# Norm sums over the partitions for two channel chunks at once, and norm weights folded into the input projection, in a selective-scan and mixture-of-experts kernel on one Trainium2 core

## The chip, the cores and the metric

The kernel runs on one NeuronCore of one Trainium2 chip. Its engines run side by side, each through its own instructions in order: TensorE (PE, matrix products into PSUM, with the loads of its stationary operand listed apart as PEld), VectorE (DVE), ScalarE (ACT), GpSimd (POOL) and SyncE (SP, which issues most of the transfers). [...] The metric is the time of one execution on the device in microseconds. Before the change the median of three runs is 3180.68 us (3179.35 to 3183.71).

## The reference

Two layers, each followed by a layer norm without weights. The first is a selective state-space model on `x` of 8 sequences, 1024 time steps and 256 features. The second sends each of the 8192 tokens to two of eight experts of limited capacity. Cut to what matters here:

```python
var = jnp.mean(x * x, axis=-1, keepdims=True)
xn = x * jax.lax.rsqrt(var + 1e-06) * norm_w
proj = xn @ W_in.T                       # 256 -> 1024: x_branch and gate
...
def step(h, inp):                        # h: (B, 512 channels, 16 states)
    dA_t, dB_t, x_t, C_t, t = inp
    h = h * dA_t + dB_t * x_t[:, :, None]
    nrm = jnp.sqrt(jnp.sum(h * h, axis=(1, 2), keepdims=True))
    fac = jnp.minimum(20.0 / (nrm + 1e-08), 1.0)
    h = jnp.where(t % 10 == 0, h * fac, h)
    y = jnp.einsum('bdn,bn->bd', h, C_t) + D_param * x_t
    return (h, y)
```

At every tenth step the state of a sequence is scaled down when its norm, taken over all 512 channels and 16 states, exceeds 20. After the scan come the gating, the output projection, the residual, the layer norm and the experts.

## The kernel before

**Tiling.** Channels lie on the 128 partitions, in `NC` = 4 chunks. Time is cut into 52 windows of 20 steps (`TW`), each window into two stretches of 10 steps (`CH`), so that the norm falls between two stretches. The eight sequences form `G` = 2 groups of `NB` = 4. A unit is one stretch of one group; it has four scans on DVE, one for each chunk, each over 16 states x 4 sequences x 11 slots (`scan`, L968, L975, L980). A window has four units.

**Order.** Nothing is scheduled by a tool. Each piece of work is put on a list with a time written out by hand (`WHEN`, `FIRST`, `LAST`), in units of one scan, and the list is sorted; that fixes each engine's order. Windows overlap: while window w is scanned, the next one is normed, projected and convolved, and the one before is gated, projected out and normed.

**Set-up.** SP issues the transfers in this order: the small parameters `sm`, the first window's `x`, the first half of `w_in` (the x branch), the convolution's biases, `w_bc`, `w_dt`, the second half of `w_in` (the gate), `w_out`, the router's weights, and a fill of `seg_d` with zeros. DVE then builds the convolution's 16 diagonal matrices `taps` from the identity and `sm` (L510), and the small constants, among them `scl`: one DVE instruction (L523), an exponential on ACT (L524), and further DVE instructions. After them come the scalings of `w_dt_sb` and `w_bc_sb` (L530 to L532).

**One window, ahead of its scans.** `rms` squares and sums on ACT (L610), takes the power on POOL (L605, L606) and scales on ACT (L614). `turn` transposes on PE into a PSUM tile `ptr` (L625). `turned` copies it to SBUF, one ACT instruction for each of the two chunks of features, with the norm's weights as a scale for each partition (L635). `project` multiplies by `w_in_sb` (L647), in four parts: two for the x branch, two for the gate. `branch` copies the x branch on ACT (L664), `convolve` runs on PE (L692, L696), `convolved` on ACT and DVE (L709, L711). `find_bc`, `find_dt` (L718, L785) and what follows give the step widths; `tanhs` and `expand` on ACT (L851, L930) give the decays. `gate` is one ACT and one DVE instruction for each half (L681, L683). All PSUM tiles called `mm` share two buffers, so a new one waits for the reader of the one before the last.

**The norm of a unit.** `norm` has five steps at times of their own: the squares of the last states on POOL (L892); their sums over the partitions on PE, as products with a matrix of ones, one for each chunk, added up in one PSUM tile of 64 columns (L897); the sum over the 16 states on DVE, giving four numbers per partition (L904); scale and power -1/2 on POOL (L909, L910); a copy into PSUM on ACT (L914). The next unit of the same group reads it in L975. The norms ahead of the first scan are in `first_states`, with the squares on DVE.

**After the scans.** POOL multiplies by C (L998), PE sums over the states (L1017) and adds the skip term (L1026), DVE multiplies by the gate (L1031), and `leave` projects out, norms and writes (L1056 to L1147). Every 256 time steps a batch of routing runs, with indirect transfers on POOL's queue (L301).

## Time and profile before

One execution was profiled. Its own time was 3200.79 us and the span of its instructions 3199.1 us, beside the 3180.68 us median of the runs without profiling.

| | us |
|---|---|
| median of three runs | 3180.68 |
| profiled execution: time, span | 3200.79, 3199.1 |
| mean granted TensorE clock, share of full | 0.944 |
| scans on DVE, L980 x824 | 1327.7 |
| norm's sums on PE, L897 x1632, 128x64 each | 219.2 (0.280 each) |
| their idle time ahead on PE | 40.4 |
| norm's reduction on DVE, L904 x204 | 0.215 median each |
| copies of the transposed norm on ACT, L635 x104 | 0.393 median each |

A line of a timeline has the start, the duration, the engine, the source line, the operation with its output and inputs, their shapes, and how many instructions of the kind follow each other; in brackets the idle time of the engine ahead of it, and whose work ended that. A float32 product shows as two PE instructions, so four products are eight. In a table by stretches, each engine has its busy time and its instructions; then follow the granted clock of PE, the share of the transfer engines, and GB/s. In the list of waits the numbers are the total in us, the times it happened, and the longest.

### The profile page before, as it was taken

The numbers are of one execution on the slowest core, as the hardware profiler recorded it, in microseconds if no ns is written. First come the engines' busy times: TensorE is split into PE (matmuls) and PEld (weight loads), VectorE is DVE, ScalarE is ACT, GpSimd is POOL, SyncE is SP. The second block draws the span as 40 slices with busy tenths as digits, with TensorE's granted clock in tenths as the row PEclk, the third lists the DMA queues.
The fourth block names the chain that finished last, engine by engine and source line by source line (L and its number), as shares of the span: only waits on it lengthen the run. The fifth ranks groups of instructions, "written<-read, shape, count | busy, mean of one in ns | idle before, by whom it ended". The sixth has DMA issues, their size and how long they took to land. (4 is left out here: it accounts for less than half of the span.)

```text
span 3199.1 us, 53115 instructions
## 1 busy us (share of the span) xinstructions
PE 2804.9 (88%) x17774; PEld 2553.2 (80%) x17774; DVE 2606.0 (81%) x3954; ACT 2435.9 (76%) x6300; POOL 2421.1 (76%) x2801
## 2 busy tenths in 40 slices
PE   5889999898898999988898999998999988579998
PEld 5788888888788888888888888887888887457666
DVE  3899999998779999998899998998899998534444
ACT  6999899998778999988899988988898986011111
POOL 2777777788987777879987877789877876856663
PEclk8899999999899999999999999999999998789999
DMA  2122222223222222222222222222222221223331
GB/s 83 60 70 65 78 66 75 70 64 70 56 54 80 65 71 72 65 70 64 68 66 72 69 71 65 74 63 69 62 76 69 63 76 51 87 71 112 121 114 50
DMA packets 167102, 229.38 MB, mean 72 GB/s; under 512 B 52948, under 2 KB 105260, under 8 KB 166828
## 3 DMA queue, kind: packets, MB, share of 16 engines
q1 hardware_dynamic: 152236, 201.48, 21.2%
q0 software_dynamic: 14592, 24.52, 3.0%
q8 instruction: 139, 2.28, 0.3%
q14 instruction: 135, 1.11, 0.1%
HBM read 185.17 MB, written 40.63 MB: 71 GB/s over the span
## 5 line engine op out<-in xcount | busy, mean ns | idle before, releaser
L980 DVE TENSOR_TENSOR_SCAN U<-dA,u 128x704 f32<-128x704 f32 (+1 forms) x824 | 1327.7, 1611 | 42.6 <-DVE u L975 0.5
L998 POOL TENSOR_TENSOR U<-U,cb 128x640 f32<-128x640 f32 x816 | 1168.6, 1443 | 96.4 <-DMA cb<-c_d 93.5
L851 ACT ACTIVATE th<-dt,a 128x160 f32<-128x160 f32 (+1 forms) x3328 | 1146.3, 422 | 0.1
L1017 PE MATMUL py<-U,ident 128*128 128x160 f32 (+1 forms) x6592 | 1058.7, 312 | 55.1 <-DVE sg L1031 50.2
L1017 PEld LDWEIGHTS py<-U,ident 128*128 128x128 f32 x6592 | 973.1, 199 | 68.1 <-DVE sg L1031 57.6
L968 DVE TENSOR_TENSOR u<-pdt,bb 128x640 f32<-128x640 f32 (+1 forms) x824 | 677.9, 823 | 39.1 <-ACT pdt L914 23.0
L930 ACT ACTIVATE dA<-th 128x640 f32<-128x640 f32 (+1 forms) x824 | 595.3, 731 | 1.6
L647 PE MATMUL pp<-xnT,w_in_sb 128*128 128x168 f32 (+1 forms) x1664 | 299.4, 328 | 11.7 <-ACT xnT L635 11.7
L692 PE MATMUL pc<-xb,taps 128*128 128x168 f32 (+1 forms) x1664 | 275.9, 309 | 21.0 <-POOL xb L663 10.5
L647 PEld LDWEIGHTS pp<-xnT,w_in_sb 128*128 128x128 f32 x1664 | 273.3, 209 | 15.3 <-ACT xnT L635 15.3
L785 PE MATMUL pd<-xc,w_dt_sb 128*128 128x168 f32 (+1 forms) x1664 | 275.0, 322 | 0.0
L692 PEld LDWEIGHTS pc<-xb,taps 128*128 128x128 f32 x1664 | 249.4, 193 | 25.3 <-POOL xb L663 12.3
L785 PEld LDWEIGHTS pd<-xc,w_dt_sb 128*128 128x128 f32 x1664 | 255.8, 201 | 0.5 <-issue 0.5
L897 PE MATMUL total<-sq,ones 128*128 128x64 f32 x1632 | 219.2, 280 | 40.4 <-POOL sq L892 35.8
L897 PEld LDWEIGHTS total<-sq,ones 128*128 128x128 f32 x1632 | 216.3, 202 | 47.8 <-POOL sq L892 45.2
L975 DVE SCALAR_TENSOR_TENSOR u<-pdt,U 128x64 f32<-128x64 f32 x816 | 222.2, 272 | 28.2
L910 POOL TENSOR_TENSOR f<-f,mhalf 128x4 f32<-128x4 f32 x204 | 209.5, 1027 | 17.0
L892 POOL TENSOR_TENSOR sq<-U 128x256 f32<-128x256 f32 x204 | 131.8, 646 | 98.4 <-DVE U L980 81.0
L1056 PE MATMUL po<-w_out_sb,sg 128*80 128x256 f32 (+1 forms) x824 | 196.7, 382 | 0.3 <-DVE sg L1031 0.3
L1425 PE MATMUL ph<-xeT,w1s 128*128 128x384 f32 x512 | 172.0, 493 | 10.5 <-DVE hT L1431 4.5
L773 POOL TENSOR_SCALAR dx<-xc,hd 128x168 f32<-128x168 f32 (+1 forms) x208 | 179.1, 866 | 2.6 <-PE py L1026 2.6
L1455 PE MATMUL epo<-w2s,hT 128*128 128x256 f32 x768 | 171.8, 383 | 9.2 <-issue 4.7
(227 smaller groups left out, 3347.4 us busy)
## 6 DMA issues: line engine op xcount, KB each, us to landing
bb<-b_d SPq DMA_DIRECT2D x206, 320.0 KB
cb<-c_d SPq DMA_DIRECT2D x206, 320.0 KB
w1s<-in_w SPq DMA_DIRECT2D x8, 1024.0 KB
w2s<-in_w SPq DMA_DIRECT2D x8, 1024.0 KB
xt<-in_x SPq DMA_DIRECT2D x102, 80.0 KB
v<-in_x SPq DMA_DIRECT2D x102, 80.0 KB
x_d<-v SPq DMA_DIRECT2D x102, 80.0 KB
sum_d<-v SPq DMA_DIRECT2D x102, 80.0 KB
```

What stands on the lines that cost most here:

```text
L647: nc.tensor.matmul(pp[:, i * S : (i + 1) * S], w_in_sb[:, k, o * P : (o + 1) * P], r["xnT"][:, k * S : (k + 1) * S], start=(k == 0), stop= ...
L692: nc.tensor.matmul(out_c, taps[:, c * KCONV + k, :], r["xb"][:, c, k * B : k * B + S], start=(k == 0), stop=False,)
L785: nc.tensor.matmul(r["pd"][:, c % 2 * S : (c % 2 + 1) * S], w_dt_sb[:, k, c * P : (c + 1) * P], r["xc"][:, k * S : (k + 1) * S], start=(k ...
L851: nc.scalar.activation(r["th", c][:, i, : B * n].rearrange("p (b t) -> p b t", b=B), dtv[:, c, :, 1 : 1 + n], AF.Tanh, scale=a16[:, cn : c ...
L897: nc.tensor.matmul(v.total[:, : NS * NB], ones, v.sq[:, c * NS : (c + 1) * NS].rearrange("p n b -> p (n b)"), start=(c == 0), stop=(c == N ...
L910: nc.gpsimd.tensor_tensor(v.f, v.f, mhalf, ALU.pow)
L930: nc.scalar.activation(dA.rearrange("p (n b) t -> p n b t", b=NB)[:, :, :, 1 : 1 + su], th[:, :, g * NB : (g + 1) * NB, v.t0 : v.t0 + su], ...
L968: nc.vector.tensor_tensor(uv[:, :, :, 1 : 1 + su], dtx.unsqueeze(1).to_broadcast([P, NS, NB, su]), v.bb.rearrange("p (n b t) -> p n b t", ...
L975: nc.vector.scalar_tensor_tensor(uv[:, :, :, 0], p.pf.unsqueeze(1).to_broadcast([P, NS, NB]), 1.0, p.h_last[:, c * NS : (c + 1) * NS, :], ...
L980: nc.vector.tensor_tensor_scan(v.U[:, c * NS : (c + 1) * NS].rearrange("p x b t -> p (x b t)"), v.dA[c].rearrange("p x t -> p (x t)"), u, ...
L998: nc.gpsimd.tensor_tensor(cut.rearrange("p x b t -> p (x b) t"), cut.rearrange("p x b t -> p (x b) t"), cb, ALU.mult,)
L1017: nc.tensor.matmul(v.py, ident, Uc[:, :, n, :, 0:ty], start=(n == 0), stop=False)
```

## The change

Three edits. First, in the set-up, ahead of the taps, four DVE instructions multiply the two halves of `w_in_sb`, for each of the two chunks of features, by the norm's weights, in place. Second, `turned` is one copy of both chunks without a scale. Third, step 1 of `norm` multiplies the matrix of ones by the squares of two chunks at once, so two products of 128 columns take the place of four of 64; step 2 then sums over 32 columns for each sequence in place of 16.

```diff
+        for half in range(2):
+            for k in range(KM):
+                part = w_in_sb[:, k, half * NC * P : (half + 1) * NC * P]
+                nc.vector.tensor_scalar(part, part, sm[:, S_NW + k : S_NW + k + 1], None, ALU.mult)
+
         taps = wpool.tile([P, NC * KCONV, P], F32, tag="taps", name="taps")
...
             r["xnT"] = xnT = p2.tile([P, KM * B * TM], F32, tag="xnT", name=f"xnT_{w}")
-            for k in range(KM):
-                nc.scalar.activation(
-                    xnT[:, k * S : (k + 1) * S], r["ptr"][:, k * S : (k + 1) * S], AF.Copy,
-                    scale=sm[:, S_NW + k : S_NW + k + 1],
-                )
+            nc.scalar.copy(xnT[:, : KM * S], r["ptr"][:, : KM * S])
...
-                for c in range(NC):
+                for c in range(0, NC, 2):
                     nc.tensor.matmul(
-                        v.total[:, : NS * NB], ones,
-                        v.sq[:, c * NS : (c + 1) * NS].rearrange("p n b -> p (n b)"),
-                        start=(c == 0), stop=(c == NC - 1),
+                        v.total[:, : 2 * NS * NB], ones,
+                        v.sq[:, c * NS : (c + 2) * NS].rearrange("p n b -> p (n b)"),
+                        start=(c == 0), stop=(c + 2 == NC),
                     )
             elif step == 2:
                 v.f = p2.tile([P, NB], F32, tag="f", name=f"f_{v.nm}")
                 nc.vector.tensor_reduce(
-                    v.f, v.total[:, : NS * NB].rearrange("p (n b) -> p b n", b=NB), AX.X, ALU.add
+                    v.f, v.total[:, : 2 * NS * NB].rearrange("p (n b) -> p b n", b=NB), AX.X, ALU.add
                 )
```

## The prediction

> **What bounds the kernel now.** I read the page first, then the start instruction by instruction, then the waits of VectorE (DVE), then single windows of 20 time steps.

> ```profile
> PE 2804.9 (88%) x17774; PEld 2553.2 (80%) x17774; DVE 2606.0 (81%) x3954; ACT 2435.9 (76%) x6300; POOL 2421.1 (76%) x2801
> ...
> PE   5889999898898999988898999998999988579998
> ...
> DVE  3899999998779999998899998998899998534444
> ```

> By share of busy time TensorE (PE) leads. But its mean mixes the scan phase (slices 2 to 34) with the expert phase behind it. In the scan phase DVE shows the same nines, so the waits have to decide.

> ```profile
> DVE xc L711 <- ACT xc L709: 127.8, 95, 7.5
> ...
> DVE u L968 <- ACT pdt L914: 23.0, 28, 4.2
> DVE f L904 <- PE total L897: 13.3, 10, 2.9
> ```

> Over the whole run DVE waits only 13.3 us for the sums this change rewrites. Its one large wait is L711, once per window, and L711 waits for ScalarE (ACT). In the timelines DVE otherwise runs scan after scan. From the first L711 of a window to the gating product L683 always takes 30.7 us, without a gap. From there to the next L711 the time varies. Two neighbouring windows show why:

> ```profile
> 1177.60 1.35 PE L1017 MATMUL py<-U,ident 128*128 128x160 f32 x8 [1.17 <-DVE sg L1031]
> ...
> 1180.79 0.48 PE L625 MATMUL ptr<-ident,xn 84*128 84x84 f32 x4 [1.83 <-DVE f L904]
> ...
> 1182.93 2.28 PE L647 MATMUL pp<-xnT,w_in_sb 128*128 128x168 f32 x8
> ...
> 1185.25 0.44 ACT L664 COPY xb<-pp 128x336 f32<-128x336 f32 x1 [1.36 <-PE pp L647]
> ...
> 1200.31 0.51 DVE L711 SCALAR_TENSOR_TENSOR xc<-xc,pc 128x336 f32<-128x336 f32 x1 [1.75 <-ACT xc L709]
> ...
> 1286.03 1.30 PE L647 MATMUL pp<-xnT,w_in_sb 128*128 128x168 f32 x8
> ...
> 1300.42 0.50 DVE L711 SCALAR_TENSOR_TENSOR xc<-xc,pc 128x336 f32<-128x336 f32 x1 [0.67 <-ACT xc L709]
> ```

> L683 frees a PSUM buffer, PE transposes into it (L625), ACT copies (L635), PE projects (L647), ACT copies (L664) and then works without a gap up to L709, which releases L711. The eight L647 took 2.28 us in one window and 1.30 in the other, because the granted clock was 0.50 there:

> ```profile
> 1178.30:1181.50 3.20, 1.37 (x12) 1.15 (x12) 3.14 (x5) 2.59 (x8) 3.20 (x4) 1.00 0.05 19
> 1181.50:1184.90 3.40, 3.40 (x15) 3.40 (x14) 3.30 (x6) 2.39 (x7) 3.23 (x6) 0.50 0.02 5
> ```

> The half clock follows a stretch in which PE was busy for only 1.37 of 3.20 us. So a window lasts as long as DVE's work plus one pass through PE and ACT, and that pass depends on whether PE has just been idle. Of 34 windows without routing 9 last about 49.4 us (full clock), 7 about 50.35 (half clock at +14 us, which delays L785 and so ACT L799), 16 about 50.8 (half clock at the transposes) and 2 about 51.9 (half clock twice running, as at 1952 to 1959). The mean is 50.39.

> The start, up to the first scan at 57 us, is one chain:

> ```profile
> 4.32 3.22 DVE L510 TENSOR_SCALAR taps<-ident,sm 128x128 f32<-128x128 f32 x16
> ...
> 7.80 0.20 ACT L524 ACTIVATE scl<-scl 128x1 f32<-128x1 f32 x1 [4.68 <-DVE scl L523]
> ...
> 7.91 0.40 ACT L610 ACTIVATE xn<-xt 84x256 f32<-84x256 f32 x1
> ...
> 8.03 0.51 SPq L478 DMA_DIRECT2D w_in_sb<-in_w_in  x1
> ...
> 13.82 1.23 DVE L530 TENSOR_SCALAR w_dt_sb<-w_dt_sb 128x2048 f32<-128x2048 f32 x1 [5.17 <-DMA w_dt_sb<-in_w_dt]
> ```

> ACT cannot begin the first norm (L610) before L524, and L524 waits for DVE L523, which stands behind the taps in DVE's order.

> **Part 1, the four multiplications of w_in.** They go into DVE's order ahead of the taps. The first two need the first half of w_in, the last two the second half, whose transfer is issued at 8.03, behind w_dt's. When does it land? Adding up the bytes of one-microsecond stretches, everything up to w_dt (some 1,890 KB) had moved by 12.5 us, and w_dt was seen landed at 13.82, 1.3 later. The second half of w_in ends at some 2,420 KB, moved by 14.5; with the same lag it lands at 15.8. Bounds: not before 13.82 (same queue, behind w_dt), and not after w_out behind it, 2,940 KB at 16.1, so 17.4. One multiplication of 128x512: 128 elements took 0.22 us (L531) and 2048 took 1.23 (L530), so 512 lie at 0.42; the taps, which take their factor from a column as these do, cost 0.06 more: 0.48. Two of them follow the landing, some 0.9 us; the first two are hidden by the wait (another 0.9 without it). Then L523 comes 3.31 behind the first tap and L524 0.17 later, as now: 15.8 + 0.9 + 3.31 + 0.17 = 20.2 against 7.80, **+12.4 us** (10.4 to 14.0). Queued behind the wait on DVE are the taps, L523 and with it ACT's L524 and L610, hence the norm, the projection and all behind them. Nothing covers this: PE, POOL and ACT have no other work. What now waits at 13.82 for w_dt will no longer wait, but that was off the chain. SP's queue only issues earlier relative to use. No DMA is added.

> **Part 2, the first norms.** The two groups of L897 before the first scan ran at half clock, 1.97 and 1.94 us, and lie on the chain: the power behind them holds POOL up to 44.2, then L828, for which ACT L946 idles 4.70 us. Four instructions in place of eight: at least half the time (0.98), at most four times the 0.285 of the 168-column L647 at half clock (1.14). I take 1.1, a gain of 0.85 each; the longer reductions return 0.07 each. **-1.6 us** (-1.9 to -1.4).

> **Part 3, the norm's sums in every window** (four norms each, 204 in all). PE: eight L897 of 64 columns take 0.92 us from start to next start, 0.115 each; 160 columns take 0.136. So 128 columns lie between, I take 0.115 (the nearer row is the floor of the small ones): 0.46 saved, 94 us over the run; with 0.136, 0.38. [...]

> PE's saving mostly ends in a wait: L1017 and L625 wait for DVE already. DVE: the reduction reads 128 in place of 64 elements. L904 takes 0.209 now, reductions of 128x128 (L243, L254) 0.266 and 0.279: +0.07 us. The bound above is L390's strided 0.38, +0.17. Two of the four reductions lie in the gapless 30.7 us and lengthen the window by 0.14; the other two are covered by the L711 wait (0.67 at least; without that cover they cost as much again).

> **Part 4, one copy for two (L635).** Two activations take 0.69 us together, the like copy of 128x336 (L664) 0.44: ACT saves 0.25. It counts only where ACT is gapless from L635 or earlier to L709, which is the 49.4 and 50.35 kinds; in the others L664 waits for PE.

> **Windows, summed.** 49.4 becomes 49.3; 50.8 becomes 50.9; 51.9 becomes 52.0; 50.35 becomes about 49.65 (L785's second half stands behind an L897 run at half clock, some 0.6 earlier, and 0.25 from the copy, less 0.14). With the old mix the mean falls by 0.10 us, -3.3 us over 34 windows. But PE's idle time ahead of the transposes grows: 1.17 + 1.83 becomes at least 1.63 + 1.83, in the very stretch after which the half clock came. I estimate the mix as 5, 6, 17 and 6: (5x49.3 + 6x49.65 + 17x50.9 + 6x52.0)/34 = 50.64, +0.25 a window, **+8.5 us**. [...] The other 17 windows pay +0.14 each, **+2 us**; where routing loads POOL I count no gain, since POOL barely idles there. The expert phase is untouched.

> Sum: 12.4 - 1.6 + 8.5 + 2 = **+21 us**; the profiled span goes from 3199.1 to 3220 (its time of 3200.79 stands 20 above the median of the runs, which I carry over as a constant): 3180.7 + 21 = **3202 us**, between 3190 (old mix) and 3215.

> **Rivals.** *PE is the bound* (88% speaks for it; against it, PE waits for DVE ahead of L625 in every undisturbed window, and DVE waits just 13.3 us for these sums). This is the faster side: if the earlier L897 brought every window to 49.3 us, 34 x 1.1 = 37 us are won and 13 lost: 3156; if all 94 us counted, 3100. It wins from the point where the clock stays full in over half of the windows. Chance 0.08. *PE cools in nearly every window*: one third at 52.0, the rest at 50.9, mean 51.28, 34 x 0.89 = +30 in place of 8.5: 3224. For it: the idle stretch, now longer than the 3.4 us of a cool one. Against: the same columns are streamed. Chance 0.21. *The late start is hidden*, the half of w_in landing early or the lost time regained by slack in the first windows (DVE still waits 7.5 us at 69 us): 3178 to 3190. Against: the bound of 13.82, and L610 has no other releaser. Chance 0.11. The forecast has 0.60.

> **How the numbers follow.** Changes under 0.2% (6.4 us) cannot be told from none here. Slower: forecast and cooling, 0.81. The hidden start gives 0.10 to no change and 0.01 to faster; with PE as the bound, faster is 0.09. The range 3186 to 3230 leaves out the PE rival, most of the hidden start, and the far end of the cooling (reductions at +0.17 included).

> **What would show it.** L524 starting near 20 us behind multiplications that wait for w_in's second half, and the first scan near 68; L897 in fours at about 0.12 each; L904 at 0.28; L711 still waiting for L709 once a window; more windows near 51 and 52 us. It is wrong if L524 stays near 8 us, or if PE's waits for DVE shrink while windows shorten to 49.3.

## The result and the profile after

| | before | after |
|---|---|---|
| median of four runs, us | 3181.77 (3179.35 to 3183.71) | 3203.0 (3199.23 to 3206.19) |
| ratio, with its 95% interval | | 1.0064 (1.0051 to 1.0076) |
| profiled execution: time, span, us | 3200.79, 3199.1 | 3206.19, 3204.5 |
| first scan on DVE starts at, us | 57.05 | 67.89 |
| last scan ends at, us | 2743.0 | 2768.5 |
| from there to the end of the span, us | 456.1 | 436.0 |
| mean granted TensorE clock | 0.944 | 0.937 |

The change makes the kernel 21 us slower. The two profiled spans differ by only 5.4 us, because the expert phase, which the change does not touch, took 20.1 us longer in the profiled execution of before (456.1 against 436.0). The part that the change touches ends 25.5 us later, and this execution is the slowest of its four, 3 above their median. New line numbers stand 5 above the old ones in the set-up and one above behind `turned`: L524 is now L529, L897 is L898, L1017 is L1018. The kernels of the experiments shift the lines again by a few; their lines are known by the names of the tiles.

The page of after gives the busy time of each engine, and the busy tenths of PE and DVE in 40 slices:

```profile
PE 2756.1 (86%) x16950; PEld 2486.1 (78%) x16950; DVE 2621.2 (82%) x3958; ACT 2427.4 (76%) x6248; POOL 2424.5 (76%) x2801
...
PE   4799898988789889888889889888889898759998
...
DVE  2899999998779999998899999998899998624444
```

PE lost 48.8 us of busy time (it had 2804.9), and the kernel is slower: busy PE was not the bound. The list of waits says who waited instead (total, times, longest):

```profile
DVE xc L712 <- ACT xc L710: 139.4, 95, 8.0
...
DVE u L969 <- ACT pdt L915: 31.4, 35, 4.2
...
DVE f L905 <- PE total L898: 7.8, 6, 2.5
```

DVE's one large wait, for the convolved branch, has grown from 127.8 to 139.4 us; its wait for the sums themselves has shrunk from 13.3 to 7.8. The start, in the timeline of after:

```profile
8.20 0.88 DVE L511 TENSOR_SCALAR w_in_sb<-w_in_sb,sm 128x512 f32<-128x512 f32 x2 [3.80 <-DMA w_in_sb<-in_w_in]
...
15.57 0.88 DVE L511 TENSOR_SCALAR w_in_sb<-w_in_sb,sm 128x512 f32<-128x512 f32 x2 [6.49 <-DMA w_in_sb<-in_w_in]
16.36 3.22 DVE L515 TENSOR_SCALAR taps<-ident,sm 128x128 f32<-128x128 f32 x16
...
19.86 0.20 ACT L529 ACTIVATE scl<-scl 128x1 f32<-128x1 f32 x1 [16.72 <-DVE scl L528]
19.96 0.40 ACT L615 ACTIVATE xn<-xt 84x256 f32<-84x256 f32 x1
...
49.92 1.22 PE L898 MATMUL total_first<-sq_first,ones 128*128 128x128 f32 x4 [5.92 <-DVE sq_first L893]
...
67.89 1.62 DVE L981 TENSOR_TENSOR_SCAN U<-dA,u 128x704 f32<-128x704 f32 x1
```

DVE stands 3.80 us for the first half of `w_in` and 6.49 us for the second, the taps follow them, and ACT's first work comes at 19.86 in place of 7.80: 12.06 us late. At the first scan 10.84 of it are left.

Then the windows. The start of each window's L711 (L712 after) was read from DVE's timeline in both traces; the difference to the next one is the window's length. Of the 34 windows without routing ("+14 us" is counted from the window's start; the transposes stand at +31 us; "twice running" means two stretches of 3.41 us, one behind the other):

| kind | length, us | before | predicted after | after |
|---|---|---|---|---|
| full clock | 49.3 | 9 | 5 | 3 |
| half clock at +14 us | 49.65 (before 50.35) | 7 | 6 | 1 |
| half clock at the transposes | 50.9 | 16 | 17 | 25 |
| half clock twice running | 51.8 | 2 | 6 | 5 |
| mean | | 50.39 | 50.64 | 50.87 |

This is +0.485 us a window, 16.5 us over 34. It comes from the numbers of each kind alone: with the numbers of before, the new lengths would have made the 34 windows 3.4 us shorter. The remaining windows together became 1.1 us shorter (866.9 to 865.7 us for 16 of them). What a window of the last kind looks like, in the timeline of PE after:

```profile
598.68 0.69 PE L898 MATMUL total<-sq,ones 128*128 128x128 f32 x4
601.04 1.35 PE L1018 MATMUL py<-U,ident 128*128 128x160 f32 x8 [1.67 <-DVE sg L1032]
604.24 0.79 PE L630 MATMUL ptr<-ident,xn 84*128 84x84 f32 x4 [1.84 <-DVE sg L684]
604.83 2.42 PE L1018 MATMUL py<-U,ident 128*128 128x160 f32 x8
607.03 2.45 PE L648 MATMUL pp<-xnT,w_in_sb 128*128 128x168 f32 x8
```

and the same time cut into stretches of 3.41 us (length; busy time and instructions of PE, PEld, DVE, ACT, POOL; granted clock, DMA share, GB/s):

```profile
595.70:599.11 3.41, 3.41 (x27) 3.34 (x25) 3.09 (x5) 3.37 (x4) 2.29 (x4) 1.00 0.16 50
599.11:602.53 3.42, 1.62 (x11) 1.18 (x9) 3.31 (x5) 3.42 (x7) 0.93 (x1) 1.00 0.68 228
602.53:605.94 3.41, 1.70 (x8) 1.73 (x9) 3.34 (x6) 2.29 (x6) 3.41 (x5) 0.50 0.04 14
605.94:609.35 3.41, 3.41 (x14) 3.41 (x14) 3.34 (x5) 1.48 (x5) 3.24 (x5) 0.50 0.04 14
```

PE runs out of work twice, waiting for DVE. The clock of the next stretch is half, that stretch holds the second gap, and the one behind it, with the projection of the next window (L648, 2.45 us for what takes 1.30), is at half clock too. The two gaps lasted 1.67 and 1.84 us, and the clock was 0.50 from 602.53 to 609.35.

### The profile page after: what moved, and what is told of

Same layout as the page of the kernel before. It is cut to its first block, busy times and chain, and to the rows that moved or that the text cites. A ratio compares the mean times of both kernels' runs of the same rounds, so it can differ in the third digit from the quotient of the medians.

```text
span 3204.5 us, 51371 instructions
## 1 busy us (share of the span) xinstructions
PE 2756.1 (86%) x16950; PEld 2486.1 (78%) x16950; DVE 2621.2 (82%) x3958; ACT 2427.4 (76%) x6248; POOL 2424.5 (76%) x2801
## 5 line engine op out<-in xcount | busy, mean ns | idle before, releaser
L1018 PE MATMUL py<-U,ident 128*128 128x160 f32 (+1 forms) x6592 | 1067.3, 314 | 92.1 <-DVE sg L1032 83.6
L1018 PEld LDWEIGHTS py<-U,ident 128*128 128x128 f32 x6592 | 983.1, 201 | 122.2 <-DVE sg L1032 111.5
L648 PE MATMUL pp<-xnT,w_in_sb 128*128 128x168 f32 (+1 forms) x1664 | 315.2, 340 | 5.1 <-ACT xnT L639 5.1
L648 PEld LDWEIGHTS pp<-xnT,w_in_sb 128*128 128x128 f32 x1664 | 289.3, 219 | 6.7 <-ACT xnT L639 6.2
L898 PE MATMUL total<-sq,ones 128*128 128x128 f32 x816 | 136.8, 292 | 46.8 <-POOL sq L893 42.0
L910 POOL TENSOR_SCALAR f<-f 128x4 f32<-128x4 f32 x204 | 39.7, 195 | 180.9 <-DVE f L905 169.3
L301 POOL DMA_INDIRECT seg_d<-meta,slot x128 | 151.3, 1182 | 28.1 <-issue 26.1
```

What stands on the lines that cost most here:

```text
L648: nc.tensor.matmul(pp[:, i * S : (i + 1) * S], w_in_sb[:, k, o * P : (o + 1) * P], r["xnT"][:, k * S : (k + 1) * S], start=(k == 0), stop= ...
L1018: nc.tensor.matmul(v.py, ident, Uc[:, :, n, :, 0:ty], start=(n == 0), stop=False)
```

## The experiments

The kernels of a set ran on one chip beside the kernel before. The median of before was 3224.46 us for the first set (e1 to e4), 3181.67 for the second (e5 to e8) and 3181.41 for the third (e9 to e11); only ratios are compared across sets. "Windows" below are the 34 without routing.

**e1_late: the change, with the multiplications of w_in moved back.** The first half is multiplied behind `hd`, the second at the end of the set-up.

```diff
-        for half in range(2):
-            for k in range(KM):
-                part = w_in_sb[:, k, half * NC * P : (half + 1) * NC * P]
-                nc.vector.tensor_scalar(part, part, sm[:, S_NW + k : S_NW + k + 1], None, ALU.mult)
...
+        for k in range(KM):
+            part = w_in_sb[:, k, 0 * NC * P : (0 + 1) * NC * P]
+            nc.vector.tensor_scalar(part, part, sm[:, S_NW + k : S_NW + k + 1], None, ALU.mult)
...
+        for k in range(KM):
+            part = w_in_sb[:, k, 1 * NC * P : (1 + 1) * NC * P]
+            nc.vector.tensor_scalar(part, part, sm[:, S_NW + k : S_NW + k + 1], None, ALU.mult)
```

> The changed kernel with the four multiplications of w_in moved in DVE's order: the first half's behind the small constants (behind hd), the second half's to the end of the set-up. Theory (the start is lost because DVE waits for w_in's second half ahead of the taps): ACT's exponential of scl is back at 7.8 us instead of 19.9, the first scan starts near 55.9 instead of 67.9, and the median falls by 12 from 3203 to about 3191; the windows stay as in the changed kernel (about 51 us, few of 49.3). Rival (the start's loss is made up by slack later on, and the windows alone carry the 21 us): the median stays at 3203.

Measured: 3238.85 us, ratio 1.0043 (1.003 to 1.0056). The timeline of its start:

```profile
7.81 0.20 ACT L524 ACTIVATE scl<-scl 128x1 f32<-128x1 f32 x1 [4.62 <-DVE scl L523]
...
18.46 0.74 DVE L584 TENSOR_SCALAR w_in_sb<-w_in_sb,sm 128x512 f32<-128x512 f32 x2
...
55.56 1.62 DVE L983 TENSOR_TENSOR_SCAN U<-dA,u 128x704 f32<-128x704 f32 x1
```

ACT's L524 is back at 7.81 and the first scan at 55.56: the place of the multiplications alone makes the start late, and they cost nothing behind the landing, where DVE no longer waits for it. But the kernel stays slower than before, by 14.4 us on its chip, against 21 (and 27 in e5) for the whole change. So there is a second loss. In this profile ten windows fell to half clock twice, and the mean was 51.04: part of what the start gave back went there. By the ratios the move gives back 7 us against the first comparison (1.0064) and 14 against e5 (1.0086), where the theory had 12 and the rival none.

**e2_fold: the fold alone**, with the multiplications where the change puts them and one copy in `turned`; the norm as before.

```diff
+        for half in range(2):
+            for k in range(KM):
+                part = w_in_sb[:, k, half * NC * P : (half + 1) * NC * P]
+                nc.vector.tensor_scalar(part, part, sm[:, S_NW + k : S_NW + k + 1], None, ALU.mult)
...
+            nc.scalar.copy(xnT[:, : KM * S], r["ptr"][:, : KM * S])
```

> The kernel before with the fold alone (the multiplications where the change has them, one copy in turned), the norm's sums as before. Theory: the start loses 12.1 us (first scan near 69.1), the windows keep their old mix of 49.4, 50.35 and 50.8 us and gain 0.25 in the first two kinds: 3182 + 12 - 4 = 3190. Rival (the fold also cools PE, as ACT hands over earlier): windows near 51 us as in the changed kernel, 3204.

Measured: 3233.11 us, ratio 1.0027 (1.0013 to 1.004). First scan at 69.34, 12.3 late; the windows' mean 50.25, none of them at half clock twice; they sum to 4.6 us less than before. The loss of 8.7 us is what the theory gave (3182 to 3190). The fold costs the late start and gives a little back; how much of that is the copy and how much a luckier mix of windows is taken up below.

**e3_pair: the paired sums alone.**

```diff
-                for c in range(NC):
+                for c in range(0, NC, 2):
                     nc.tensor.matmul(
-                        v.total[:, : NS * NB], ones,
-                        v.sq[:, c * NS : (c + 1) * NS].rearrange("p n b -> p (n b)"),
-                        start=(c == 0), stop=(c == NC - 1),
+                        v.total[:, : 2 * NS * NB], ones,
+                        v.sq[:, c * NS : (c + 2) * NS].rearrange("p n b -> p (n b)"),
+                        start=(c == 0), stop=(c + 2 == NC),
                     )
...
-                    v.f, v.total[:, : NS * NB].rearrange("p (n b) -> p b n", b=NB), AX.X, ALU.add
+                    v.f, v.total[:, : 2 * NS * NB].rearrange("p (n b) -> p b n", b=NB), AX.X, ALU.add
```

> The kernel before with the norm's sums for two chunks alone, no fold. Theory (a shorter L897 leaves PE idle ahead of the transposes, so that most windows run through the half clock, and DVE's longer reduction adds 0.14 a window): first scan near 55.8, windows mostly 50.9 to 52.0, mean 50.8 to 51.0, so -1.2 + 10 to 16: 3190 to 3197. Rival (all of the loss is the start): 3180.

Measured: 3241.7 us, ratio 1.0045 (1.0029 to 1.0062). First scan at 54.95, 2.1 early; the windows 0, 2, 23 and 9 of the four kinds, mean 51.09, 23.9 us more than before. The profiled run is the slowest of the six, 7.4 us above their median; the median itself lost 17.2 us where 10 to 16 were expected. The pairing, meant to take work off PE, carries the whole loss of the windows: with the fold alone they lost nothing.

**e4_wide: the longer reduction without the shorter products.** Four products of 64 columns as before, but into two halves of `total`, so that DVE sums 128 columns.

```diff
+                    at0 = c // 2 * NS * NB
...
-                        v.total[:, : NS * NB], ones,
+                        v.total[:, at0 : at0 + NS * NB], ones,
...
-                        start=(c == 0), stop=(c == NC - 1),
+                        start=(c % 2 == 0), stop=(c % 2 == 1),
...
-                    v.f, v.total[:, : NS * NB].rearrange("p (n b) -> p b n", b=NB), AX.X, ALU.add
+                    v.f, v.total[:, : 2 * NS * NB].rearrange("p (n b) -> p b n", b=NB), AX.X, ALU.add
```

> The kernel before with four products of 64 columns still, but two into columns 0 to 63 and two into 64 to 127, and the reduction over all 128: PE's work as before, DVE's reduction as after. Theory (the idle PE is the larger part of the windows' loss, the reduction the smaller): the reduction takes 0.28, L711 to L683 takes 30.84 in place of 30.70, windows keep their kinds (each 0.14 longer, some of 49.5), +5 to +7 us: 3187 to 3189. Rival (the reduction is what lengthens the windows): as with the pair alone, 3190 to 3197, with hardly any window of 49.5.

Measured: 3231.97 us, ratio 1.0017 (1.0003 to 1.0031). The groups of e4 between 400 and 2700 us (busy, mean ns of one, idle ahead):

```profile
L898 PE MATMUL total<-sq,ones 128*128 128x64 f32 x1402 | 185.4, 277 | 35.2 <-POOL sq L892 33.3 <-DVE carry L279 1.9
...
L905 DVE TENSOR_REDUCE f<-total 128x4 f32<-128x128 f32 x176 | 48.6, 276 | 11.4 <-PE total L898 11.2 <-issue 0.3
```

and of the change:

```profile
L898 PE MATMUL total<-sq,ones 128*128 128x128 f32 x700 | 116.4, 290 | 35.2 <-POOL sq L893 33.3 <-DVE carry L279 1.8
...
L905 DVE TENSOR_REDUCE f<-total 128x4 f32<-128x128 f32 x176 | 48.6, 276 | 7.2 <-PE total L898 7.1
```

The reduction is the same 276 ns in both, while PE spends 185.4 us on the products in e4 and 116.4 in the change. Its windows sum to 8.6 us more than before, of which 34 x 0.14 = 4.8 are the longer reduction itself. By these profiles the reduction is the smaller part of e3's 23.9 us, and the shorter time on PE the larger. The medians say the same less sharply: e4 lost 7.5 us (5 to 7 expected) and e3 17.2, and their intervals just overlap. The split is known no closer than that.

**e5_after: the change once more**, unedited, as the basis of the second set.

> The changed kernel itself again, beside the others of this set on one chip. Theory: 1.006 of the kernel before, first scan at 67.9, windows without routing mostly 50.9 (half clock), with three to five of 49.3 and five to ten of 51.8.

Measured: 3208.44 us, ratio 1.0086 (1.0073 to 1.01); windows 4, 1, 24 and 5, mean 50.83. The mix came back nearly the same on another chip. This profile is of the fastest of its five runs. The loss of 26.8 us is 5.5 us above the first comparison's, and the two intervals just overlap: how large the loss is, is known to some 5 us.

**e6_fill_after, e7_fill_late, e8_fill_late_fold: PE kept streaming.** If PE's idle stretch ahead of the transposes brings the half clock, products that fill it must bring the full clock back, although they are work added. Four products with a matrix of zeros, added to the sum that PE builds at that moment, stand ahead of the transposes, and two more at another place of the window, where the clock fell at +14 us. They add zero, so the output is unchanged.

```diff
+    zeros = const.tile([P, P], F32, tag="zeros", name="zeros")
+    nc.gpsimd.memset(zeros, 0.0)
...
+            extra = {(1, 1, 0): 4, (0, 1, 3): 2}.get((v.j, v.g, n0 * 4 // NS), 0)
+            for _ in range(extra):
+                nc.tensor.matmul(v.py, zeros, Uc[:, :, n0, :, 0:ty], start=False, stop=False)
```

e6 is the change with these lines, e7 is e1 with them, and e8 is e7 with the norm of before (four products, short reduction), so that of the change only the fold is left, its multiplications moved back.

> The changed kernel, with products by a matrix of zeros added into the open sum over the states: four in the unit whose L1018 comes ahead of the transposes, two in the unit ahead of the router's product. They add zero to the sum; PE is only kept streaming where it idled. Theory (the half clock after PE's idle stretch is what lengthens the windows): most windows last 49.3 to 49.5 us, the clock stays full at the transposes, 34 x 1.4 = some 45 us less than the changed kernel in the windows, 0.986 of it and 0.992 of the kernel before. Rival (the windows are longer since DVE, POOL or the norm's chain got longer, the clock only goes along): no window gets shorter than 50.9, and the time is that of the changed kernel or above.

> The same filling with the multiplications of w_in moved out of the way as in the first experiment. Theory (the start's 12 us and the windows' clock are two separate losses that add): 12 us less than with the filling alone, first scan near 55.6: 0.988 of the kernel before. Rival (the windows make up for the start, as the first experiment's saving of some 6 us instead of 12 may suggest): no less than with the filling alone.

> The filling and the moved multiplications with the norm's sums as before (four products of 64 columns, reduction over 64): the fold without its late start, and a warm PE. Theory: as the run before it, with the first scan 1.2 us later, each window 0.14 shorter on DVE's side: 7 - 1 = 6 us less, 0.986 of the kernel before. If the shorter product for two chunks has a worth of its own once PE is warm, this run is no faster than the one before.

| | us | ratio (95%) | full clock / +14 us / transposes / twice | first scan | sum of the 34 windows |
|---|---|---|---|---|---|
| e5_after | 3208.44 | 1.0086 (1.0073 to 1.01) | 4 / 1 / 24 / 5 | 67.89 | 1728.1 |
| e6_fill_after | 3144.69 | 0.9886 (0.9871 to 0.9902) | 34 / 0 / 0 / 0 | 66.73 | 1677.2 |
| e7_fill_late | 3133.84 | 0.9852 (0.9838 to 0.9865) | 33 / 0 / 1 / 0 | 55.75 | 1678.0 |
| e8_fill_late_fold | 3127.16 | 0.9836 (0.9823 to 0.985) | 33 / 0 / 1 / 0 | 57.43 | 1674.7 |

The timeline of PE in e6, at the place shown above for the change:

```profile
337.13 0.70 PE L900 MATMUL total<-sq,ones 128*128 128x128 f32 x4
339.50 1.35 PE L1020 MATMUL py<-U,ident 128*128 128x160 f32 x8 [1.66 <-DVE sg L1037]
340.69 1.25 PE L1025 MATMUL py<-U,zeros 128*128 128x160 f32 x8
342.69 0.48 PE L632 MATMUL ptr<-ident,xn 84*128 84x84 f32 x4 [0.75 <-DVE sg L686]
```

and in stretches:

```profile
338.12:341.53 3.41, 2.03 (x15) 2.04 (x16) 3.34 (x5) 3.41 (x8) 2.39 (x2) 1.00 0.67 172
341.53:344.94 3.41, 2.66 (x21) 2.45 (x21) 3.34 (x6) 2.59 (x8) 3.24 (x7) 1.00 0.02 5
344.94:348.36 3.42, 3.42 (x27) 3.42 (x26) 3.35 (x5) 3.42 (x11) 3.42 (x4) 1.00 0.10 40
```

The gap of 1.84 has become 1.25 of streaming and 0.75 of idling, PE's busy time in the two stretches is 2.03 and 2.66 us in place of 1.62 and 1.70, and the clock stays full. None of the 34 windows has a half clock at either place. Nothing is released earlier by the added products themselves; the gain of 64 us over e5 (3208.44 - 3144.69) comes from the clock, whose mean over the profiled execution is 0.969 in e6 and 0.935 in e5. The 34 windows gave 51 us of it, where the theory had 45; the other windows shrank too (16 of them from 864.6 to 855.3 us), which was not followed further. e7 against e6 gives the late start by itself, without the noise of the mix: 10.85 us. e8 against e7 gives the pairing with PE kept at full clock: a net loss of 6.7 us. It gains 1.7 us up to the first scan (55.75 against 57.43) and loses 8.2 from there to the last, 3.3 of them in the 34 windows and 5.0 in the 13 with routing. So the shorter products have no worth of their own in the windows, and the longer reduction costs. e8 is 1.6% faster than the kernel before and the fastest of all.

**e9_fill_elsewhere: the control**, as many zero products in the change, at two other places of the window.

```diff
-            extra = {(1, 1, 0): 4, (0, 1, 3): 2}.get((v.j, v.g, n0 * 4 // NS), 0)
+            extra = {(0, 0, 1): 4, (1, 0, 1): 2}.get((v.j, v.g, n0 * 4 // NS), 0)
```

> The changed kernel with the same six products by zeros for each window, but put where PE does not idle: four in the unit after the one ahead of the transposes, two in the third unit. Control for the filling. Theory (what counts is streaming in the idle stretch): no gain, windows of 50.9 and 51.8 as in the changed kernel, 1.007 to 1.010 of the kernel before. Rival (any added streaming keeps the clock up): as the filling, 0.99.

Measured: 3202.95 us, ratio 1.0063 (1.0047 to 1.008); windows 4, 2, 27 and 1. Its PE, ahead of the transposes:

```profile
344.30 1.35 PE L1020 MATMUL py<-U,ident 128*128 128x160 f32 x8 [1.21 <-DVE sg L1037]
...
347.50 0.48 PE L632 MATMUL ptr<-ident,xn 84*128 84x84 f32 x4 [1.84 <-DVE sg L686]
```

The gap of 1.84 us ahead of the transposes is still there, and so is the loss of time. The theory had 1.007 to 1.010, the rival 0.99. What counts is the place of the added work, not its amount.

**e10_fill_before: the kernel before with the same filling** as e6.

> The kernel before with the filling, without any part of the change. Theory (ACT's 0.25 us of the merged copy counts in every window once PE is warm, and the fold costs nothing when its multiplications are out of the way): windows of 49.4 us, 34 x 0.25 = some 8 us above the fold with moved multiplications and filling, the first scan at 57: 0.986 of the kernel before. Rival (the fold is worth nothing): 0.9836, as the run with the fold.

Measured: 3139.68 us, ratio 0.9867 (0.985 to 0.9883); windows 33, 0, 1 and 0. The kernel before had the same weakness, with 42 us in it. Against e8 (0.9836, an interval that just touches this one) it shows what the fold is worth when its multiplications don't stand ahead of the taps: 0.31%, some 10 us by the medians and 8 by the ends of the last scan in the two profiles; a window at full clock takes 49.18 us in place of 49.38.

Against e6 it shows how much of the change's loss went through the clock. Both filled, the change stands 0.0019 behind the kernel before (0.9886 and 0.9867, some 6 us, with intervals that overlap); without the filling it stands 0.0064 to 0.0086 behind (21 to 27 us). So some 15 to 21 us of the loss are the clock's. What is left is about the late start and the net cost of the pairing, 10.85 and 6.7, less the 8 to 10 that the fold gains.

**e11_fill_turn: the change, filled at the transposes alone.**

```diff
-            extra = {(1, 1, 0): 4, (0, 1, 3): 2}.get((v.j, v.g, n0 * 4 // NS), 0)
+            extra = {(1, 1, 0): 4}.get((v.j, v.g, n0 * 4 // NS), 0)
```

> The changed kernel with the four products ahead of the transposes alone, not the two ahead of the router's product. Theory (two separate places cool): the windows of 50.9 and 51.8 go, but some of 49.7, cooled at +14 us, stay among those of 49.3: some 5 us above the filling at both places, 0.990 of the kernel before. If the second place never mattered in the changed kernel: 0.9886.

Measured: 3149.77 us, ratio 0.989 (0.9873 to 0.9906). One window still cools at the transposes (50.38 us); 15 of the 34 cool at +14 us, most of them 0.35 us longer. By the sums of the windows the second filling is worth 5.7 us (1682.9 against 1677.2), which is what the theory gave; the ratios alone can't tell it from the rival, as their intervals overlap.

## Why the prediction was right

**The start, +12.4.** Right in its mechanism and size. `w_in`'s second half was seen landed at 15.57 (15.8 estimated); two multiplications took 0.79 us from start to the taps' start (0.9); L524 moved by 12.06. e1 and e7 show that their place in DVE's order is the whole cause. At the first scan 10.84 of it are left; the rest is the next term, with 0.1 of scatter.

**The first norms, -1.6.** The two groups took 1.22 and 1.19 us in place of 1.97 and 1.94, a gain of 0.75 each where 0.85 was taken. From the first of these products to the first scan the time fell from 19.33 to 17.97 us, by 1.36: two gains of 0.75, less 0.07 twice for the reductions. In e3, which has the pairing alone, it is 17.99, in e4 19.49.

**PE's products, 0.46 less a norm.** A group of four, where PE has no wait, takes 0.61 us in place of 1.00, so 0.39, between the 0.38 and 0.46 that were given: from start to start an instruction of 128 columns takes 0.111 us and one of 64 0.104, nearly the same. (The 0.115 of the prediction was read from a longer row than most: from the first start to the next instruction's, the median group of eight takes 0.84 us, not 0.92.) Over the run 219.2 became 136.8 us, and as was said, the saving ended in a wait: PE's idle time ahead of L1018 with DVE's gating as the releaser grew from 50.2 to 83.6 us. The rival that PE bounds the kernel falls with that: 82 us less of its work gave nothing.

**The reduction, +0.07; the gapless part, +0.14.** 0.209 became 0.276, and from L711 to the gating product 30.70 became 30.83. In e8 against e7 an undisturbed window is 0.11 longer (49.29 against 49.18); the 0.14 for each of the other windows was too little there, 5.0 us in 13.

**The copy, -0.25.** Two at 0.69 became one of 0.44. It was said to count in the first two kinds of windows alone, and there it did: in e2 they are 49.21 and 50.14 us long in place of 49.41 and 50.35. The windows cooled at the transposes became 0.10 longer (50.77 to 50.87), which was not followed, so that with the old mix e2's 34 windows would have gained only 1.6 us of their 4.6; the rest is the mix.

**The mix of windows, +8.5.** This is the term that was mis-sized: it measured +16.5. The lengths of the kinds were right within 0.2 us; the numbers of each were an estimate, and 30 windows cooled at the transposes where 23 were expected. The reason given, that the time PE saves lengthens its idle time in the stretch that decides the clock, is what e3, e6 and e9 show (0, 34 and 4 of the 34 windows at full clock). By e6 and e10 the clock's part of the loss is some 15 to 21 us, which fits. The rival of a PE that cools in nearly every window was nearly right in how many cool, and wrong that a third of them would cool twice: five did, and the mean of 50.87 lies nearer to the forecast's 50.64 than to the rival's 51.28.

**The other windows, +2.** They became 1.1 us shorter; the sign was wrong, by 3 us.

**The expert phase, carried over.** The prediction took the 20 us by which the profiled execution before stood above the median for a constant and expected a profiled span of 3220 us. It was 3204.5: from the last scan to the end the profiled execution of before took 456.1 us, and that of after 436.0. So the 20 us were no constant; the forecast of the median doesn't rest on them.

The terms as measured, 10.8 + 16.5 - 1.1, give 26.2 where the last scan moved by 25.5 in the profiled execution, which is 3 us above its median. The forecast had 21.3 for the same terms, and the medians lie 21.2 apart. So the direction, the late start and the cooling were foreseen, but the agreement of 3203.0 with 3202 to the microsecond is luck: the mix was given half its size, the other windows the wrong sign, the runs of after lie 7 us apart, and e5 shows the same kernel 5 us further from before.

**Still open:** why one occasion draws more windows of one kind than another (e1 had ten that cooled twice, the change five), what shortens the windows with routing when PE is filled, and how e3's loss is divided between the shorter products and the longer reduction.

## What to carry to other kernels

Where an engine's clock depends on how busy it has been (here 0.50 behind a stretch with PE busy for 1.62 of 3.42 us), taking work off it can cost time: look at what the saved time turns into, and whether it falls into a stretch that is already half idle. Before optimising such an engine, see if the work behind its idle stretches runs at a lower clock; here a few products with zeros in that place made the kernel before 1.3% faster (e10) and the changed one 2.0% (e6 against e5), while the pairing, with over a third less PE work on the sums (219.2 to 136.1 us), lost 0.45% (e3). And an in-order engine's set-up should hold nothing ahead of the critical chain that waits for a late transfer: the same four multiplications cost 11 us in one place and nothing in another.

## What was not expected of the hardware

The busy time in one cell tells what follows better than the length of a gap. Of the cells of after between 102 and 2730 us that had the full clock, those with PE busy for 1.6 us or less were followed by half clock 47 times in 49, those with over 2.0 us 2 times in 587; in between it was 14 of 51. In before the counts are 34 of 37, 1 of 627 and 15 of 35. Gaps of nearly the same length, 1.8 to 1.9 us at full clock, led to half clock 36 times in 42 in after and 23 in 33 in before. So gaps of the same length may or may not be followed by half clock; that it depends on how the grid cuts them is the author's reading of these counts. A window cooled at the transposes lasts 50.9 us, nearly 15 cells (51.2), so the next window meets the grid at nearly the same place. That would explain why such windows follow one another in rows; it is only argued here, no run tested it.
